# Loading a batch's attention operands from DRAM in two transfers with a doubled source instead of eight

## The chip, the cores and the metric

The kernel runs on one core of one Trainium2 chip. The metric is the device time of one execution in microseconds (us). Three runs of the kernel before took 4955.44, 4955.54 and 4960.33 us; the median is 4955.54 us.

A core has a matrix engine (TensorE, PE in the profile), three engines for elementwise work (VectorE or DVE, ScalarE or ACT, GpSimd or POOL) and a sync engine (SP). In this kernel SP alone issues the transfers between DRAM and the on-chip memory; 16 DMA engines carry them out.

## The reference

32 batches pass through four layers, with queries of shape 112 x 256 and a context of 375 x 256 per batch. The last layer (L3) is what matters here. It has 16 heads of size 16, a causal self-attention, a cross-attention over the context and a feed-forward block:

```python
def _mha(q_in, kv_in, wq, bq, wk, bk, wv, bv, causal):
    q = jnp.einsum('btc,hcd->bhtd', q_in, wq) + bq[None, :, None, :]
    k = jnp.einsum('bsc,hcd->bhsd', kv_in, wk) + bk[None, :, None, :]
    ...
    scores = jnp.einsum('bhtd,bhsd->bhts', q, k) * q.shape[-1] ** (-0.5)
    ...
x = x + _mha(ln1(x), ln1(x), ..., causal=True) @ m_proj_w + m_proj_b
x = x + _mha(ln2(x), x_e, ..., causal=False) @ c_proj_w + c_proj_b
x = x + relu(ln3(x) @ f_w1 + f_b1) @ f_w2 + f_b2
```

(The normalisations are written short here.)

## The kernel before

The kernel goes through nine sweeps over all batches: `l0x`, `l1s`, `l1x`, `l1f`, `l2x`, `l2f`, `l3s`, `l3x`, `l3f`. The first digit is the layer; `s` is self-attention, `x` cross-attention, `f` feed-forward. Batches are taken two at a time (`GB = 2`). Some sweeps run beside another one, staggered (`PAIRS`): `l2f` with `l3s`, and `l3x` with `l3f`.

Each sweep is cut into slots, and a slot into phases: scores and softmax, normalisation, transposition, product with the values, projection. `run` lays the slots of all sweeps in one sequence. `LAGS` says by how many slots a later phase trails the first. Preparatory steps (loading x, statistics, projections, loading operands) are "atoms"; `LEAD` says how many slots ahead of its unit each atom is due. For `l3s` the queries are loaded 3 slots ahead (`qload=3`), for `l3x` 4 slots (`qload=4`) and the keys 8 (`kload=8`). After this planning the framework's own scheduler, which works with a modelled timeline, decides the final order on each engine and the waits.

In L3, a value is kept as a high and a low part, so that a float32 product keeps its precision: a score is the sum of high x high, high x low, low x high and low x low. With heads of size 16 all four products are made in one matmul over 128 partitions. For each pair of heads `m`, the 128 partitions hold 8 blocks of 16 rows: two heads (`j`) and four combinations of query part and key part. Query rows of the other head of the pair are zeros.

To bring the operands into this form the kernel goes through DRAM. `queries_out` (line 854) writes the two parts of the projected queries of a batch pair into a DRAM buffer `dq_l3s` or `dq_l3x`, three buffers in turn, whose other rows were filled with zeros once. `queries_in` (line 871) reads a batch's queries back into a tile `qs` of 128 partitions x 2 x 8 x 112, with eight transfers (line 879): for each head parity `j` and each part `q`, the same 32 rows twice (`u`). The partitions so hold (high, high, low, low), in blocks of 32. `keys_out` (line 838) writes the keys to DRAM, and `keys_in` (line 845) reads them into two tiles `k6`, each by two transfers of 64 rows (line 852); the partitions hold (high, low, high, low).

`queries_in` is called once per batch in `l3s` and in `l3x`. `keys_in` is called once per batch pair in `l3s` (from the buffer `dk`, rows of 4 x 224 values) and once per batch in `l3x` (from `k3_...`, rows of 4 x 376 values, written during `l3s`). There are two `qs` buffers and five `k6` buffers.

The scores are then made on TensorE in line 1163 (`l3s`) and line 1111 (`l3x`):

```python
q, k = st["q"](2 * pr + j), st["k"](pr)
self.mark[s] = nc.tensor.matmul(sc[:, :TE], q, k, start=True, stop=True)
```

Other transfers run on the same SP queue in these sweeps. `keep_v` in line 521 stores the `l3x` values of each batch as two transfers of 125 rows, and line 1037 loads them again. Line 516 loads the kept context (`cd`), line 842 stores keys, line 868 stores queries, line 385 loads x, line 396 stores x. Elsewhere, lines 502 and 750 store and load values in 125 rows, line 552 stores the context in 128 rows, and line 269 loads eight bias vectors, each with its one row read twice (`partition_broadcast(2)`).

Of the kernel before, what the change touches and what calls it, by code (L numbers as in the profile page):

```python
# [8 lines left out]
F32 = mybir.dt.float32  # L9
# [52 lines left out]
class Kern:  # L62
# [775 lines left out]
    def keys_out(self, hl, W, tag, bufs):  # L838
# [3 lines left out]
            self.nc.sync.dma_start(d[:, j].rearrange("q d m n -> (d m) q n").bitcast(F32), hl[j].bitcast(F32))  # L842
        return d

    def keys_in(self, d, W):

        n = 4
        ts = [self.t([128, n, W], F32R, "k6") for _ in range(8 // n)]
        src = d.rearrange("q j d m n -> (q j d) m n")
        for ti, t in enumerate(ts):  # L850
            for u in range(2):
                self.nc.sync.dma_start(t[64 * u : 64 * u + 64].bitcast(F32), src[:, ti * n : (ti + 1) * n, :].bitcast(F32))
        return lambda m: ts[m // n][:, m % n, :]

    def queries_out(self, hl, s):
# [15 lines left out]
    def queries_in(self, d, i):  # L871

        t = self.t([128, 2, 8, S], F32R, "qs")
        for j in range(2):
            for q in range(2):
                src = d[i, j, q].rearrange("j d m n -> (j d) (m n)").bitcast(F32)
                for u in range(2):
                    o = 64 * q + 32 * u
                    self.nc.sync.dma_start(t[o : o + 32, j].rearrange("p m n -> p (m n)").bitcast(F32), src)
        return lambda hd: t[:, hd % 2, hd // 2, :]  # L880

    def queries_apart(self, i, c, bs):
# [717 lines left out]
```

## Time and profile before

| | |
|---|---|
| median of three runs | 4955.54 us |
| time of the profiled execution | 4969.08 us |
| span of the profiled execution | 4967.3 us |
| mean granted TensorE clock | 0.958 |
| TensorE busy, matmul / weight load | 4502.3 us (91%) / 4010.3 us (81%) |
| DVE / ACT / POOL busy | 73% / 69% / 43% |
| DMA: bytes, share of 16 engines (main queue) | 667.40 MB, 53.5% |
| transfers from `dq_l3s` / `dq_l3x` into `qs` | 256 / 256, 112.0 KB each |
| transfers from `dk` into `k6` | 64, 224.0 KB each |
| transfers from `k3_...` into `k6` | 128, 376.0 KB each |
| issue of one query transfer on SP, median | 419 ns |

How to read it: the page gives each engine's busy time as a share of the span, so an engine at 91% has little idle time left on average, though single stretches differ. The strips of digits cut the span into 40 slices of 124 us. The DMA share is the mean over 16 engines: a share of 0.31 can mean five engines that are busy all the time. GB/s is what all of them moved. In tile names buffer numbers are left out, so `k` stands for tiles of several kinds; `k<-dk` are the key loads of `l3s`, `k<-k` holds those of `l3x` (128) and the key stores before them (64). In the view of the DMA queues of a stretch, packets are counted by size. A row of a transfer is one packet, and completions are packets under 512 B; such views count the packets that start in the stretch, while issues are those of SP in it.

### The profile page before, as it was taken

The numbers are of one execution on the slowest core, as the hardware profiler recorded it, in microseconds if no ns is written. First come the engines' busy times: TensorE is split into PE (matmuls) and PEld (weight loads), VectorE is DVE, ScalarE is ACT, GpSimd is POOL, SyncE is SP. The second block draws the span as 40 slices with busy tenths as digits, with TensorE's granted clock in tenths as the row PEclk, the third lists the DMA queues.
The fourth block names the chain that finished last, engine by engine and source line by source line (L and its number), as shares of the span: only waits on it lengthen the run. The fifth ranks groups of instructions, "written<-read, shape, count | busy, mean of one in ns | idle before, by whom it ended". The sixth has DMA issues, their size and how long they took to land. (4 is left out here: it accounts for less than half of the span.)

```text
span 4967.3 us, 111690 instructions
## 1 busy us (share of the span) xinstructions
PE 4502.3 (91%) x37824; PEld 4010.3 (81%) x37824; DVE 3625.6 (73%) x9806; ACT 3409.2 (69%) x10644; POOL 2112.1 (43%) x3674
## 2 busy tenths in 40 slices
PE   5999999997778888888999999998998986899999
PEld 5888888886667777777999999997888886788878
DVE  4788888888887777776688888886555554677776
ACT  4788888887777766775577777774544544677776
POOL 4455555555443333332233333334333333566665
PEclk9999999999889999999999999999999998899999
DMA  4433333335666667667355555543656657666663
GB/s 102 124 85 86 84 80 88 86 87 127 135 141 134 138 128 135 129 143 143 110 142 143 142 142 143 143 128 108 196 172 198 189 182 212 174 160 165 160 165 85
DMA packets 585414, 674.53 MB, mean 136 GB/s; under 512 B 318688, under 2 KB 495056, under 8 KB 584656
## 3 DMA queue, kind: packets, MB, share of 16 engines
q1 hardware_dynamic: 584848, 667.40, 53.5%
q8 instruction: 305, 5.00, 0.4%
q14 instruction: 261, 2.14, 0.1%
HBM read 323.55 MB, written 173.02 MB: 100 GB/s over the span
## 5 line engine op out<-in xcount | busy, mean ns | idle before, releaser
L217 POOL TENSOR_SCALAR k<-k,sm 112x375 f32<-112x375 f32 (+1 forms) x1536 | 931.8, 619 | 1025.2 <-DVE sm L646 453.9
L200 ACT ACTIVATE k<-ps 125x336 f32<-125x336 f32 (+4 forms) x2005 | 912.8, 468 | 416.1 <-PE ps L237 190.1
L606 DVE TENSOR_REDUCE sm<-sc 112x1 f32<-112x375 f32 x1792 | 941.7, 539 | 151.8 <-PE sc L773 87.2
L612 ACT ACTIVATE k<-sc,sm 112x375 f32<-112x375 f32 x1536 | 879.5, 578 | 116.0 <-DVE sm L606 97.4
L664 PE MATMUL ps<-ident,k 112*125 112x112 f32 x4608 | 737.5, 277 | 19.8 <-issue 4.1
L664 PEld LDWEIGHTS ps<-ident,k 112*125 112x125 f32 x4608 | 649.9, 190 | 78.8 <-issue 41.8
L773 PE MATMUL sc<-k,qs 128*112 128x376 f32 x2048 | 540.0, 356 | 18.5 <-ACT k L612 8.3
L235 PE MATMUL ps<-w,k 128*125 128x256 f32 (+2 forms) x1344 | 435.6, 324 | 32.0 <-ACT k L612 17.9
L235 PE MATMUL ps<-h,w 128*128 128x224 f32 x1408 | 411.9, 300 | 44.0 <-DVE h L202 17.2
L695 DVE TENSOR_TENSOR k<-ps,k 64x376 fp32r<-64x376 f32 x640 | 350.0, 547 | 121.3 <-ACT k L200 106.0
L236 PE MATMUL ps<-h,w 128*128 128x224 f32 x1408 | 397.3, 284 | 0.7 <-DVE h L231 0.3
L237 PE MATMUL ps<-h,w 128*128 128x224 f32 x1408 | 395.0, 283 | 0.0
L236 PE MATMUL ps<-w,k 128*125 128x256 f32 (+2 forms) x1344 | 393.1, 292 | 0.0
L202 DVE COPY k<-ps 125x336 f32<-125x336 f32 (+2 forms) x619 | 289.0, 467 | 141.5 <-PE ps L237 65.2
L237 PE MATMUL ps<-w,k 128*125 128x256 f32 (+2 forms) x1344 | 391.9, 292 | 0.0
L235 PE MATMUL ps<-k,w 128*128 128x376 f32 x896 | 343.2, 383 | 37.2 <-DMA k<-cd 25.4
L213 POOL TENSOR_SCALAR k<-k,sm 112x375 f32<-112x375 f32 x256 | 164.5, 643 | 467.0 <-DVE sm L646 287.8
L795 PE MATMUL ps<-k,k 125*64 125x112 f32 (+1 forms) x4608 | 349.8, 296 | 3.7 <-DVE k L202 1.6
L773 PEld LDWEIGHTS sc<-k,qs 128*112 128x112 f32 x2048 | 304.4, 177 | 47.3 <-ACT k L612 23.5
L235 PEld LDWEIGHTS ps<-h,w 128*128 128x128 f32 x1408 | 275.0, 199 | 70.9 <-issue 28.9
L235 PEld LDWEIGHTS ps<-w,k 128*125 128x125 f32 (+2 forms) x1344 | 266.9, 199 | 72.7 <-ACT k L612 29.3
L612 ACT ACTIVATION_READ_ACCUMULATOR k<-sc,sm 112x1 f32 x1536 | 322.5, 210 | 0.0
(213 smaller groups left out, 12623.3 us busy)
## 6 DMA issues: line engine op xcount, KB each, us to landing
qs<-h SPq DMA_DIRECT2D x512, 224.0 KB
k<-k SPq DMA_DIRECT2D x192, 376.0 KB
k<-cd SPq DMA_DIRECT2D x64, 752.0 KB
vd<-k SPq DMA_DIRECT2D x128, 375.0 KB
k<-vd SPq DMA_DIRECT2D x128, 375.0 KB
qs<-dq_l3s SPq DMA_DIRECT2D x256, 112.0 KB
qs<-dq_l3x SPq DMA_DIRECT2D x256, 112.0 KB
x<-xd SPq DMA_DIRECT2D x224, 112.0 KB
```

The costliest lines, as they stand in the source:

```text
L200: self.nc.scalar.activation(out, in_, AF.Identity)
L202: self.nc.vector.tensor_copy(out, in_)
L217: self.nc.gpsimd.tensor_scalar(out, in_, by, 1.0, ALU.mult, ALU.mult)
L235: mm(out, lhs(0), rhs(0), start=start, stop=False)
L236: mm(out, lhs(0), rhs(1), start=False, stop=False)
L237: mm(out, lhs(1), rhs(0), start=False, stop=stop)
L606: nc.vector.tensor_reduce(nms[j], sc[j][:, :n], AX.X, ALU.max, negate=True)
L612: nc.scalar.activation(p[:, j, :n], sc[j][:, :n], AF.Exp, bias=nms[j], scale=1.0 if scale is None else scale, accum_out=sm[:, j : j + 1])
L664: self.nc.tensor.transpose(pst[:TB, a * S : (a + 1) * S], p[:, j, a * TB : (a + 1) * TB], self.ident[:S, :S])
L695: nc.vector.tensor_tensor(ks[o, j, :], pk[r, :TE], ks[r, j, :].bitcast(F32), ALU.subtract)
L773: nc.tensor.matmul(sc[:, :TE], qs[:, hd, q, bs], kk, start=q == 0, stop=q == 1)
L795: nc.tensor.matmul(o if gqa else o[:, mm, :], vq[:, a, hd * 64 : hd * 64 + 64], st["pt"][:, :, j, ta] if gqa else st["pt", mm][:, j, ta], ...
```

## The change

`keys_in` and `queries_in` exchange their layouts. The queries' partitions hold (high, low, high, low) in blocks of 32, the keys' (high, high, low, low). All four products are still there once. A new function `twice` makes one transfer whose source is the given DRAM rows with a dimension of 2 and step 0 put in front, so that the rows are read twice and fill the destination's partitions one copy after the other. `queries_in` then makes two transfers of 128 destination partitions, where it made eight of 32. `keys_in` still makes four of 64 destination partitions, each now of 32 source rows read twice.

```diff
+    def twice(self, out, src):
+
+        r, n = src.shape
+        self.nc.sync.dma_start(
+            out.bitcast(F32), src.bitcast(F32).unsqueeze(0).to_broadcast([2, r, n])
+        )
+
     def keys_in(self, d, W):
 
         n = 4
         ts = [self.t([128, n, W], F32R, "k6") for _ in range(8 // n)]
-        src = d.rearrange("q j d m n -> (q j d) m n")
         for ti, t in enumerate(ts):
-            for u in range(2):
-                self.nc.sync.dma_start(t[64 * u : 64 * u + 64].bitcast(F32), src[:, ti * n : (ti + 1) * n, :].bitcast(F32))
+            for q in range(2):
+                self.twice(
+                    t[64 * q : 64 * q + 64].rearrange("p m n -> p (m n)"),
+                    d[q].rearrange("j d m n -> (j d) m n")[:, ti * n : (ti + 1) * n, :].rearrange("p m n -> p (m n)"),
+                )
         return lambda m: ts[m // n][:, m % n, :]
...
         t = self.t([128, 2, 8, S], F32R, "qs")
         for j in range(2):
-            for q in range(2):
-                src = d[i, j, q].rearrange("j d m n -> (j d) (m n)").bitcast(F32)
-                for u in range(2):
-                    o = 64 * q + 32 * u
-                    self.nc.sync.dma_start(t[o : o + 32, j].rearrange("p m n -> p (m n)").bitcast(F32), src)
+            self.twice(t[:, j].rearrange("p m n -> p (m n)"), d[i, j].rearrange("q j d m n -> (q j d) (m n)"))
         return lambda hd: t[:, hd % 2, hd // 2, :]
```

## The prediction

> **What bounds the kernel now.** I read the page first, for the shape of the run.
>
> ```profile
> span 4967.3 us, 111690 instructions
> PE 4502.3 (91%) x37824; PEld 4010.3 (81%) x37824; DVE 3625.6 (73%) x9806; ACT 3409.2 (69%) x10644; POOL 2112.1 (43%) x3674
> DMA  4433333335666667667355555543656657666663
> ...
> qs<-dq_l3s SPq DMA_DIRECT2D x256, 112.0 KB
> qs<-dq_l3x SPq DMA_DIRECT2D x256, 112.0 KB
> ```
>
> TensorE is busy 91% of the span; the transfers use about half of the 16 DMA engines. The last two rows are the loads that the change rewrites. By the line's own view they are issued from 3456.5 to 4208.4 us (l3s) and from 4168.9 to 4894.4 us (l3x), so everything touched lies in the last third. I then asked for the stretches before, during and after.
>
> ```profile
> 3450.00:4180.00 730.00, 638.72 (x5200) 583.19 (x5199) 376.96 (x1052) 352.34 (x1433) 259.69 (x452) 0.92 0.63 192
> 4180.00:4895.00 715.00, 643.50 (x6718) 558.87 (x6718) 520.63 (x1469) 496.33 (x1594) 414.27 (x656) 0.94 0.64 166
> 4895.00:4967.00 72.00, 68.35 (x735) 63.99 (x734) 39.86 (x111) 45.60 (x141) 36.82 (x57) 1.00 0.09 28
> ```
>
> After the length, the columns are the busy us of PE, PE's weight load, DVE, ACT and POOL, then granted clock, DMA share, GB/s. TensorE is busy 87 to 90% here; the DMA share is 0.63, averaged over 16 engines. The waits of TensorE from 3450 us on say what a perfect query load could save:
>
> ```profile
> PE sc L1163 <- DMA qs<-dq_l3s: 36.9, 12, 5.1
> PE ps L235 <- DMA k<-cd: 25.4, 6, 10.9
> ```
>
> So 36.9 us is lost to queries, in 12 waits. This part is bound by TensorE, with DMA at two thirds of its capacity if every transfer uses all engines. Whether it does is seen in three stretches with few transfers in flight, in the view of the DMA queues.
>
> ```profile
> DMA packets 144, 0.77 MB, mean 220 GB/s; under 512 B 16, under 2 KB 16, under 8 KB 144
> ...
> q1 hardware_dynamic: 144, 0.77, 54.5%
> ...
> cd<-k SPq DMA_DIRECT2D x1, 752.0 KB
> ```
>
> That is 1140 to 1143.5 us: one store of 128 rows. 144 packets are 128 rows and 16 small ones, one for each engine that reports completion. The second is 1472.4 to 1477.6 us, one store of 125 rows (the transpose beside it was issued 0.45 us before the end):
>
> ```profile
> DMA packets 130, 0.38 MB, mean 74 GB/s; under 512 B 5, under 2 KB 5, under 8 KB 130
> ...
> q1 hardware_dynamic: 130, 0.38, 24.4%
> ...
> vd<-k SPq DMA_DIRECT2D x1, 375.0 KB
> ```
>
> 125 rows and 5 completions: five engines, since 5 is the largest divisor of 125 up to 16. The third is 191 to 200 us, in which the eight bias loads of line 269 are issued and land. Each reads one 1 KB row twice, through a source whose outermost count is 2 with step 0:
>
> ```profile
> DMA packets 814, 0.83 MB, mean 92 GB/s; under 512 B 35, under 2 KB 813, under 8 KB 813
> ...
> k<-in_ctx_dram SPq DMA_DIRECT2D x1, 375.0 KB
> xh<-in_L_xattn_a_bo_dram SPq DMA_DIRECT2D x2, 2.0 KB
> ```
>
> Eight loads on 16 engines would leave 128 completions. There are 35 in all, some of them of transfers issued earlier and of the 125-row context load. Two per load fit, sixteen do not. The number of engines follows the outermost count of the transfer.
>
> **The change, part by part.** TensorE, DVE, ACT and POOL issue the same numbers of instructions in the built program; the scheduler moves 459 of them on PE, 168 on DVE, 45 on ACT and 32 on POOL, all from the start of l3s on. SP issues 384 transfers fewer: 128 query loads for 512. Only SP issues transfers, so no other queue is passed.
>
> Saved issue time: 384 x 0.419 us (the median on line 879) = 161 us of SP, worth on the end only what it takes from the waits just shown, at most 36.9 us.
>
> The form of the transfers is what costs. In the built program the query load's source is 2 copies (step 0) x 64 rows x 896 values, its destination 128 partitions; a key load's source is 2 copies x 32 rows, its destination 64 partitions. The outermost source count is 2 for all of them, as in line 269. I therefore take two engines for every one, where the old forms (32 and 64 rows on both sides) divide by 16. What remains unshown: no load in this trace has a count of 2 on one side and 128 on the other, so the sides' roles are a rival below.
>
> The Trainium skill, "DMA: Bandwidth & Descriptors", section "Why a DMA increments its semaphore by 16 and not by 1", speaks to that gap: the engine count is the largest number up to 16 that divides the slowest non-1 count of both patterns. Its section "Rules for kernel authors" warns that a leading zero-stride broadcast of c copies confines the whole DMA to at most c engines, so by that page the sum is the two-engine one below; the same section's advice against splitting a load by partition halves would, taken alone, make it the 16-engine one. The 125-row and the two-copy loads above agree with the first rule; unequal counts no row here shows.
>
> Bytes on the two engines. Queries: 512 x 112 KB = 58.7 MB. Keys: 64 loads of 224 KB and 128 of 376 KB = 64.0 MB. Together 122.7 MB, 61.3 MB on each of two engines. From 3450 us on the kernel moves 261.0 MB (140.17 and 120.86 in the DMA views of 3450 to 4180 and 4180 to 4967 us); 138.3 MB are left, of which 128 transfers of 375 KB (v3, 125 rows, five engines) are 49.2 MB, 9.8 per engine, and the rest 89.2 / 16 = 5.6 MB per engine. I let the five include my two, since the bias loads, issued by 196.5 us behind a five-engine context load, were landing up to the end of that view. So 76.8 MB pass through each of the two.
>
> Rate of one engine. The 128-row store: 0.77 MB in 0.545 x 16 x 3.5 us of engine time = 25.2 GB/s. The 125-row store: 0.384 / (0.244 x 16 x 5.2) = 18.9. Two 125-row loads with little beside them (2564.7 to 2572 us, 0.74 MB at a share of 26.7%): 23.7. All of 4180 to 4967 us, all engines contending: 119.5 MB / (0.583 x 16 x 787) = 16.3. With two engines at work there is little contention, so I take the middle of 23.7 and 25.2, 24.45, and keep 16.3 and 25.2 as ends.
>
> 76.8 MB / 24.45 = 3139 us, against 1438 us in which these loads are issued today. Nothing covers the difference: TensorE has 1351 us of work there and would idle. Buffers (two for queries, five for keys) let a batch's loads run beside the batch before, so I add only the exchange that no buffer covers: per pair of batches and stage, the queries' write to DRAM must land before the read; in the chain of waits its pieces (2.77, 3.47, 4.06, 4.87 us) average 3.8, times 32 = 121 us. Below nothing this cannot be; its upper end is a quarter of the transfer time, if buffers also run dry.
>
> What queues behind: SP's issue stalls when the engines are full (eight query loads issued at 3464.06 us took 10.98 us, not 3.4), so x, v and the stores wait in SP's order, and with them all engines. The moved instructions I price at nothing: they sit inside the idle time; without that cover they are bounded by today's TensorE slack in the part, 1517 - 1351 = 166 us, either way.
>
> Sum: start 3456.5 + 3139 + 121 + tail after the last query load (4967.3 - 4894.4 = 72.9) = 6789 us of span. The profiled execution took 4969.08 us, 1.8 over its span and 13.5 over the median of 4955.54, so 6777, told as **6780 us**, 37% slower.
>
> **Rivals.**
>
> *Sixteen engines after all* (other sign). If the destination's 128 partitions decide the split, the loads spread evenly and the change does what it looks like: the 36.9 us, 3.7 of l3x and 1.3 of keys go, 4955.5 - 41.9 = 4914 us; half of it if the loads stay late for other reasons, 4935. For: no row has unequal counts. Against: the eight bias loads. It decides from eight engines up, where 122.7 / 8 + 15.4 = 30.7 MB at 24.45 take 1257 us, less than 1438.
>
> *Two engines at a lower rate.* At 18.9 GB/s: 4061 us, 7712 of span, 7700 told. At 16.3: 4709 us, 8350 told. For: copies of the same rows are read side by side, and loads contend today. Against: two engines leave the memory nearly idle.
>
> *Two engines, but hidden.* It needs 76.8 MB in 1438 us, 53 GB/s per engine, twice the best row. Excluded.
>
> *Two engines, v elsewhere.* (61.3 + 5.6) / 25.2 = 2655 us and no exchange: 6185 of span, 6170 told.
>
> **How the numbers follow.** Two engines near my rate: 65%. Lower rate (7300 and over): 14%. V elsewhere or better overlap (under 6400): 13%. Sixteen: 8%, of which 6% gain over 0.2%, 1% stay within 0.2% (what a measurement can tell from no change) and 1% lose. Chances: faster 0.06, same 0.01, slower 0.93. The range reaches from the end at 6170 to the 18.9 row's 7700: it leaves out the 8% and the slowest tenth.
>
> **What would show it.** Step 1: in any stretch of l3s or l3x the DMA share falls from 0.63 to some 0.2 and the rate from 190 to some 70 to 90 GB/s; small packets fall, as each new load leaves 2. Step 2: until 3450 us nothing changes. Step 3: TensorE's longest waits become query and key loads (over 1000 us in all), busy near 67%. Step 4: SP's issues on the new line take many us each. I am wrong if the share stays above 0.5 there, or if the part is under 2600 us long.

## The result: 37% slower, as forecast

The changed kernel takes 6800.87 us (median of four runs, 6788.95 to 6807.92), against 4956.51 us for the kernel before in the same session. The ratio is 1.3702, with a 95% interval of 1.3683 to 1.3721. The forecast was 6780 us, with a range of 6150 to 7700.

### The profile after

The page, its strips, and the rows of the query loads:

```profile
span 6787.2 us, 111215 instructions
PE 4675.5 (69%) x37824; PEld 4154.7 (61%) x37824; DVE 3631.5 (54%) x9806; ACT 3415.1 (50%) x10644; POOL 2111.0 (31%) x3674
...
PEclk9999999899999999999977777776666666666667
DMA  4433334666666645455423333332211111111111
...
DMA packets 574787, 674.47 MB, mean 99 GB/s; under 512 B 308064, under 2 KB 484432, under 8 KB 574032
...
qs<-dq_l3s SPq DMA_DIRECT2D x64, 448.0 KB
qs<-dq_l3x SPq DMA_DIRECT2D x64, 448.0 KB
```

Each digit of a strip now stands for 170 us. The first twenty slices, up to 3400 us, are those of before, drawn shorter. From there on the DMA share falls to 0.2 to 0.3 and then to 0.1, and TensorE falls with it to a third or a half. The packets under 512 B are the main line here. The page of before has:

```profile
DMA packets 585414, 674.53 MB, mean 136 GB/s; under 512 B 318688, under 2 KB 495056, under 8 KB 584656
```

So there were 318688 of them and now there are 308064, that is 10624 fewer. (Not all of them are completions: data rows of 448 bytes, 32768 in either trace, are counted too, and drop out of the difference.) The old kernel had 512 query and 192 key loads (704); the new one has 128 and 192 (320). If the old ones left 16 completions each and the new ones 2, the difference is 704 x 16 - 320 x 2 = 10624. It fits to the last packet.

The two engines can be seen at work in the view of the DMA queues from 5024 to 5039 us, in l3x, where only query loads move data (212 rows of 3584 bytes are the 0.76 MB):

```profile
DMA packets 214, 0.76 MB, mean 51 GB/s; under 512 B 2, under 2 KB 2, under 8 KB 214
...
q1 hardware_dynamic: 214, 0.76, 12.4%
```

12.4% of 16 engines are 1.98 engines. They move 51 GB/s, 25.5 GB/s each (0.76 MB in 0.124 x 16 x 15 us), and the two small packets are the completions of one load. The stretches of l3s and l3x (3452 to 4857 and 4857 to 6787 us) in the columns of the prediction:

```profile
3452.00:4857.00 1405.00, 691.87 (x5265) 627.96 (x5263) 387.22 (x1076) 362.29 (x1475) 262.83 (x456) 0.72 0.31 102
4857.00:6787.00 1930.00, 828.80 (x7333) 720.33 (x7332) 553.62 (x1546) 534.41 (x1685) 444.56 (x703) 0.66 0.17 60
```

The same stretches of work took 751 us (3452 to 4203) and 764 us (4203 to 4967) in the kernel before. The number of instructions per engine is the same; the time is not work. What TensorE waits for from 3440 us on:

```profile
PE sc L1116 <- ACT k L612: 427.9, 35, 46.3
PE sc L1168 <- DMA k<-dk: 427.0, 17, 44.2
PE sc L1116 <- DMA qs<-dq_l3x: 256.2, 33, 15.3
PE ps L664 <- ACT k L200: 205.7, 6, 35.5
PE ps L235 <- DMA k<-cd: 176.9, 16, 24.3
```

Three of these rows name transfers (with `k<-v`, 130.6 us, and `qs<-dq_l3s`, 48.4 us, such rows come to 1039 us). The two rows that name ScalarE lead to transfers as well, since ScalarE was itself waiting. The page's rows of these two lines (behind the second bar stand the idle time of the engine before them and what ended most of it):

```profile
L612 ACT ACTIVATE k<-sc,sm 112x375 f32<-112x375 f32 x1536 | 878.6, 577 | 818.3 <-DMA dq_l3x<-k 474.5
L200 ACT ACTIVATE k<-ps 125x336 f32<-125x336 f32 (+4 forms) x2005 | 912.5, 468 | 686.9 <-DMA dq_l3x<-k 249.7
```

`dq_l3x<-k` are the stores of the queries to DRAM, for which the same two lines waited 4.9 and 5.5 us before. They stand in SP's order behind the loads. One case: SP stands 12.91 us at a load (line 848) from 5522.65 us on and only then issues the stores (line 877); the last piece of them takes 13.95 us from 5542.48 us on, and TensorE, which had waited 33.7 us for ScalarE, goes on at 5557 us. SP shows how a load now holds up what stands behind it (the line's own view: ns, shortest, median, longest issue):

```profile
L848 SPq DMA_DIRECT2D k<-k x128: 482/4276/14544, 4688.8 to 6685.3; - x128
...
L848 SPq DMA_DIRECT2D qs<-dq_l3x x64: 482/3918/12643, 4800.6 to 6695.3; - x64
```

A query issue took 419 ns in the median before. Now SP stands some 4 us at an issue in l3x, and up to 14.5. The 704 query and key loads of before held SP for 330 us in all, the 320 of now for 1460 us: 384 issues fewer cost far more of SP's time.

### The profile page after: what moved, and what is told of

Same layout as the page of the kernel before. It is cut to its first block, busy times and chain, and to the rows that moved or that the text cites. A ratio compares the mean times of both kernels' runs of the same rounds, so it can differ in the third digit from the quotient of the medians.

```text
span 6787.2 us, 111215 instructions
## 1 busy us (share of the span) xinstructions
PE 4675.5 (69%) x37824; PEld 4154.7 (61%) x37824; DVE 3631.5 (54%) x9806; ACT 3415.1 (50%) x10644; POOL 2111.0 (31%) x3674
## 2 busy tenths in 40 slices
DMA packets 574787, 674.47 MB, mean 99 GB/s; under 512 B 308064, under 2 KB 484432, under 8 KB 574032
## 4 chain that ended last, share of the span: by engine, by line
DMA 28%; PE 23%; SPq 12%; DVE 2%; issue 1%; ACT 0%; POOL 0%; ACTq 0%; DVEq 0%; POOLq 0%
DMA qs<-dq_l3x 10%; SPq L848 7%; DMA qs<-dq_l3s 5%; DMA dq_l3x<-k 4%; PE ps L664 3%; PE ps L235 3%; DMA k<-dk 3%; PE ps L236 3%; PE ps L237 3%; PE sc L773 2%; PE ps L795 2%; DMA out_dram<-x 2%; SPq L1042 1%; PE ps L1080 1%; SPq L385 1%
## 5 line engine op out<-in xcount | busy, mean ns | idle before, releaser
L664 PE MATMUL ps<-ident,k 112*125 112x112 f32 x4608 | 785.5, 290 | 221.3 <-ACT k L200 208.2
L664 PEld LDWEIGHTS ps<-ident,k 112*125 112x125 f32 x4608 | 696.3, 203 | 286.2 <-issue 252.7
L1116 PE MATMUL sc<-k,qs 128*112 128x376 f32 x512 | 208.5, 429 | 716.6 <-ACT k L612 427.9
L1116 PEld LDWEIGHTS sc<-k,qs 128*112 128x112 f32 x512 | 100.5, 205 | 741.6 <-ACT k L612 446.0
L773 PE MATMUL sc<-k,qs 128*112 128x376 f32 x2048 | 540.2, 356 | 19.4 <-ACT k L612 9.3
L231 POOL TENSOR_TENSOR ot<-s,ot 128x224 fp32r<-128x224 f32 x224 | 152.6, 683 | 1139.9 <-ACT ot L200 633.1
L235 PE MATMUL ps<-k,w 128*128 128x376 f32 x896 | 348.7, 389 | 189.1 <-DMA k<-cd 176.9
L235 PE MATMUL ps<-h,w 128*128 128x224 f32 x1408 | 425.0, 309 | 53.3 <-DVE k L931 17.5
L1168 PE MATMUL sc<-k,qs 128*112 128x112 f32 x512 | 100.1, 326 | 475.4 <-DMA k<-dk 427.0
L236 PE MATMUL ps<-h,w 128*128 128x224 f32 x1408 | 411.6, 294 | 0.6 <-DVE h L231 0.3
L237 PE MATMUL ps<-h,w 128*128 128x224 f32 x1408 | 409.1, 293 | 0.0
L1168 PEld LDWEIGHTS sc<-k,qs 128*112 128x112 f32 x512 | 83.0, 214 | 491.7 <-issue 248.2
L222 ACT ACTIVATE s<-ps,vec_L_xattn_b 128x224 f32<-128x224 f32 x128 | 58.2, 459 | 596.8 <-PE ps L237 596.5
```

What stands on the lines that cost most here:

```text
L235: mm(out, lhs(0), rhs(0), start=start, stop=False)
L236: mm(out, lhs(0), rhs(1), start=False, stop=False)
L237: mm(out, lhs(1), rhs(0), start=False, stop=stop)
L664: self.nc.tensor.transpose(pst[:TB, a * S : (a + 1) * S], p[:, j, a * TB : (a + 1) * TB], self.ident[:S, :S])
L773: nc.tensor.matmul(sc[:, :TE], qs[:, hd, q, bs], kk, start=q == 0, stop=q == 1)
```

## The experiments

Theory A is that of the prediction: a transfer runs on as many engines as the outermost count of its source allows, 2 in the changed kernel, and the time follows from the bytes on the fullest engine. Theory B puts the loss on the new layout, on the moved instructions or on fewer and larger transfers. Theory C says that any source with a step of 0 is slow.

### The layout without the doubled source

```diff
-                self.twice(
+                self.copies(          # keys: 8 transfers of 32 rows per batch
...
-            self.twice(t[:, j]...
+            self.copies(t[:, j]...    # queries: 4 transfers of 64 rows per batch
+    def copies(self, out, src):
+        r = src.shape[0]
+        for u in range(2):
+            self.nc.sync.dma_start(out[r * u : r * u + r].bitcast(F32), src.bitcast(F32))
```

> The new layout kept, but each doubled transfer is made as two plain ones (queries 4 of 64 rows per batch, keys 8 of 32 rows), so no source has a copy count in front. Theory A (a doubled source with the 2 outermost runs on two engines): 16 engines again, DMA share above 0.5 and some 160 to 200 GB/s from 3450 us on, time within 1% of 4956 us. Theory B (the cost is in the layout, in the moved instructions of the other engines or in fewer and larger query transfers): stays near 6800 us, or at least above 5500.

Measured: 5009.19 us, ratio 1.0102 (1.0077 to 1.0127). The 37% are gone with the doubled source, so the new layout does not make them. The page has 317664 small packets, 1024 fewer than before, which is 704 x 16 - 640 x 16 for the 640 loads of this run: sixteen engines each. Fewer and larger transfers, the other part of theory B, are settled by the run with the copies inside below. The 1.0% that is left is a little over what theory A allowed. It lies in l3s, whose last key store is issued at 4236.9 us instead of 4200.4. There TensorE's wait for the context loads grew; its row from 3440 us on, 25.4 us before, is now the one below. Why it grew was not tried.

```profile
PE ps L235 <- DMA k<-cd: 93.4, 15, 10.8
```

### Only the queries, only the keys

```diff
# only the queries doubled: the keys' call becomes plain
-                self.twice(
+                self.copies(
...
# only the keys doubled: the queries' call becomes plain
-            self.twice(t[:, j]...
+            self.copies(t[:, j]...
```

> Only the queries use the doubled source; the keys are plain loads of 32 rows. Theory A: 58.7 MB instead of 122.7 lie on two engines. With 9.6 MB of evenly spread bytes and 9.8 MB of the 125-row transfers that is 48.8 MB per engine, 1995 us at 24.45 GB/s, told 5640 us (5450 to 5850). Theory B': the number of query issues is at fault: as the changed kernel, 6800 us.

> Only the keys use the doubled source; queries are plain loads of 64 rows. Theory A: 64.0 MB on two engines. In l3s 7.3 MB of keys, 6.2 of the rest and 4.9 of 125-row transfers are 18.5 MB per engine, 755 us, about what that part takes from TensorE; in l3x 24.6 + 2.9 + 4.9 = 32.4 MB, 1325 us instead of 715. Told 5600 us (5450 to 5800), nearly all of the loss behind 4200 us. Theory B (layout or order): no such split by part.

Measured: 5794.87 us for the queries (1.1686, 1.1651 to 1.1721) and 5927.75 us for the keys (1.1954, 1.1919 to 1.1989). Either half alone makes a large loss, in the direction that the bytes say, and the small packets fit two engines for the doubled half and sixteen for the plain one (4864 and 6784 fewer than before, 704 x 16 - 128 x 2 - 384 x 16 and 704 x 16 - 256 x 16 - 192 x 2). But both times lie above the forecasts: by 155 us, inside the range, and by 328 us, outside it. The parts show where. I take the issue of the last key store of l3s as its end, in the view of line 842 (last number ahead of the semicolon), for the kernel with doubled keys:

```profile
L842 SPq DMA_DIRECT2D k<-k x64: 359/388/5197, 3496.2 to 4470.3; - x64
```

It was 4200.4 us before and 4855.0 in the changed kernel. So with doubled keys l3s takes some 1018 us, where the two engines have 755 us of transfers and the part took 748 us before. l3x takes 1460 us, against 1398 by bytes and tail. The forecast had nearly all of the loss in l3x; 270 us of it lie in l3s.

Part of both misses is the rate of an engine, which the length of each packet in the trace's records gives. With doubled queries, the query rows of l3x (3584 bytes, the only ones of that size there) took 164 ns on average, 21.8 GB/s, against 145 ns and 24.8 GB/s in the changed kernel. At 21.8 GB/s the 48.8 MB of the forecast take 2239 us, not 1995. With doubled keys, the key rows of l3x (6016 bytes) took 258 ns, 23.4 GB/s; at that rate 32.4 MB take 1385 us, with the tail about the 1460 measured. What makes l3s some 263 us longer than its 755 us of transfers is not shown: rows of keys and of queries have the same size there and can't be told apart.

### The copies inside instead of in front

```diff
     def twice(self, out, src):
         r, n = src.shape
         self.nc.sync.dma_start(
-            out.bitcast(F32), src.bitcast(F32).unsqueeze(0).to_broadcast([2, r, n])
+            out.bitcast(F32), src.bitcast(F32).unsqueeze(1).to_broadcast([r, 2, n])
         )
...
             for q in range(2):
-                self.twice(t[64 * q : 64 * q + 64]..., d[q]...)
+                self.nc.sync.dma_start(
+                    t[64 * q : 64 * q + 64].rearrange("p m n -> p (m n)").bitcast(F32),
+                    d.rearrange("c j d m n -> (j d) c m n")[:, :, ti * n : (ti + 1) * n, :].rearrange("p c m n -> p c (m n)").bitcast(F32),
+                )
```

Queries now hold each row in two neighbouring partitions, keys hold their two parts in neighbouring partitions. The number of transfers and their bytes are those of the changed kernel; the queries still have a step of 0.

> The same number of transfers as the changed kernel (2 for queries, 4 for keys) and the same bytes, but the copies lie inside: the query source is 64 rows, each read twice in a row (rows outermost, then the 2 with step 0); keys are 32 rows times their two parts. The partitions hold the same four products in another order. Theory A: the outermost count is 64 or 32, so all 16 engines work: 4920 to 4970 us; with the query waits (36.9 us) gone at best 4915. Rival C (any source with a step-0 dimension, wherever it stands, is slow, for instance because the same row is read twice side by side): above 5600 us.

Measured: 4907.94 us, ratio 0.9891 (0.9864 to 0.9917); run again later, 4917.07 us and 0.9913 (0.9889 to 0.9937). Theory C falls: the step of 0 does not slow a load that has 64 rows in front of it. What was left of theory B falls too, since the number and the bytes of the transfers are those of the changed kernel. Its page has 312544 small packets, 6144 fewer than before, which is 704 x 16 - 320 x 16: all sixteen engines report. This version is about 1% faster than the kernel before, 12 us under the range that was expected, and close to the 4914 us that the prediction worked out for sixteen engines. TensorE's waits for query loads, 36.9 + 3.7 us before, have shrunk to these two rows:

```profile
PE sc L1168 <- DMA qs<-dq_l3s: 0.8, 1, 0.8
...
PE sc L1116 <- DMA qs<-dq_l3x: 0.5, 1, 0.5
```

### Four and eight copies in front

```diff
-            out.bitcast(F32), src.bitcast(F32).unsqueeze(0).to_broadcast([2, r, n])
+            out.bitcast(F32), src[: 2 * r // 4].bitcast(F32).unsqueeze(0).to_broadcast([4, 2 * r // 4, n])
```

and the same with 8 in place of 4.

> The changed kernel with 4 copies of half the source rows in front (a step-0 count of 4): the same transfers and bytes, but each destination row gets a row of the first half, so the low parts (queries) or the second head of each pair (keys) are left out of the scores. Theory A (the engine count is the outermost count): four engines. 122.7 / 4 + 15.4 = 46.1 MB per engine, 1885 us at 24.45 GB/s, told 5520 us (5350 to 5750); 4 completions per transfer; DMA share about 0.3 and rate near 100 GB/s in l3x. Rival C (a step-0 dimension in front costs the same whatever its count): 6800 us. Rival D (any small count makes the transfer fall to a fixed two engines): 6800 us.

> As the kernel with 4 copies, with 8 copies of a quarter of the source rows; three quarters of the rows are left out of the scores. Theory A: eight engines, 122.7 / 8 + 15.4 = 30.7 MB per engine, 1257 us, less than TensorE's 1351 us in this part, so the loss is all but gone: 4900 to 5100 us. Rivals C and D: 6800 us.

Measured: 5621.85 us with four copies (1.1325, 1.1255 to 1.1394) and 5167.11 us with eight (1.0409, 1.0334 to 1.0484). With two copies it is 6801, with 64 or 32 rows in front 4908. Rivals C and D, that the count does not matter or that a small one always gives two engines, are out. The page with four copies:

```profile
DMA packets 575427, 674.47 MB, mean 120 GB/s; under 512 B 308704, under 2 KB 485072, under 8 KB 574672
```

318688 - 308704 = 9984 = 704 x 16 - 320 x 4: four completions for each load. With eight copies the page has 309984 small packets, 8704 fewer, which is 704 x 16 - 320 x 8. Four copies came out 100 us over the forecast and inside its range; eight came out 67 us above its range. The views of l3x show why, first with four copies, then with eight:

```profile
4437.00:5625.00 1188.00, 765.22 (x7330) 665.47 (x7326) 552.33 (x1545) 532.88 (x1684) 442.18 (x701) 0.77 0.28 98
4250.00:5156.00 906.00, 727.42 (x7322) 635.21 (x7320) 551.02 (x1545) 532.92 (x1684) 442.43 (x702) 0.88 0.44 129
```

A busy engine moved 98 / (0.28 x 16) = 22 GB/s with four copies and 129 / (0.44 x 16) = 18 with eight. It was 22 with two (60 GB/s at a share of 0.17) and 16 in the kernel before (152 at 0.59, from 4203 to 4967 us). The forecast for eight took 24.45 GB/s, so that 1257 us would hide behind TensorE's work. At 18 GB/s its 30.7 MB are some 1700 us, and the part took 1704 us (3452 to 5156).

### Where the gain of the copies inside comes from

```diff
# cut by destination partitions: 4 transfers of 64 partitions per batch
+            for q in range(2):
+                self.twice(t[64 * q : 64 * q + 64, j]..., d[i, j, q].rearrange("j d m n -> (j d) (m n)"))
# cut by columns: 4 transfers of 128 partitions, half a row each
+            for w in range(2):
+                n = slice(4 * S * w, 4 * S * w + 4 * S)
+                self.twice(t[:, j]...[:, n], d[i, j]...[:, n])
```

> The kernel with the copies inside once more, as a yardstick for the two variants beside it: 4890 to 4920 us, some 1% under the kernel before.

> Copies inside as in the yardstick, but the query transfers are cut by destination partitions: 4 per batch, each of 64 partitions (32 rows, each twice in a row), 16 engines each. Theory G (the gain of the yardstick over the kernel before comes from loads that fill all 128 partitions at once, against the old loads of 32): part of the gain is lost, 4920 to 4945 us. Theory H (it comes from fewer issues on SP): the same as the variant cut by columns, 4910 to 4930 us for both.

> Copies inside as in the yardstick, the query transfers cut by columns: 4 per batch, each of 128 partitions and half a row (1792 bytes). Theory G: as the yardstick, 4890 to 4920 us. Theory H: as the variant cut by partitions, 4910 to 4930 us.

Measured: 4917.07 us (0.9913) for the yardstick, 4959.03 us (1.0006, 0.9992 to 1.0021) cut by partitions, and 4925.64 us (0.9936, 0.9914 to 0.9957) cut by columns. The two variants make the same number of query transfers and differ by 0.7%; their intervals do not touch. So the gain is not in the number of issues alone (theory H). It goes with the 128 destination partitions (theory G), and cut into 64 nothing of it is left, less than I had forecast; cut by columns the time is 6 us above theory G's range. The 33 us between the two variants stand in TensorE's waits for transfers, from 3440 us on cut by partitions:

```profile
PE ps L235 <- DMA k<-cd: 43.7, 6, 10.8
...
PE sc L1169 <- DMA qs<-dq_l3s: 23.1, 7, 4.7
```

and cut by columns:

```profile
PE ps L235 <- DMA k<-cd: 31.8, 7, 8.8
...
PE sc L1172 <- DMA qs<-dq_l3s: 0.5, 1, 0.5
```

These rows differ by 34.5 us. That the width is the reason is argued, not shown: the order in which the scheduler put the instructions was not held fixed, and the width does not order the rates. In l3x a query row of 3584 bytes took 207 ns on average in the yardstick and 229 ns cut by partitions, but 201 ns in the kernel before, whose loads have 32 partitions. What limits the loads of 64 partitions was not tried.

### More lead in l3s

```diff
-        l3s=dict(load=10, stats=8, apply=7, q=7, qload=3, k=6, ...
+        l3s=dict(load=13, stats=12, apply=11, q=11, qload=5, k=10, ...
```

> The changed kernel with more lead in l3s: queries and keys projected 11 and 10 slots ahead instead of 7 and 6, query loads 5 instead of 3. In the changed kernel l3s took 1405 us, where its bytes on the two engines (31.3 MB at 24.45 GB/s) give 1280. If the rest is a wait for loads that start too late (427 us of TensorE's waits there name the key loads), l3s falls to about 1300 and the time to some 6690 us. If SP's fixed order behind the long issues sets it, no gain: 6800 us or more. l3x stays at some 1930 us either way.

Measured: 6796.71 us in one run, no gain. The wait for the key loads did shrink, and another took its place. TensorE from 3440 us on:

```profile
PE ps L235 <- DMA k<-cd: 591.9, 21, 43.7
...
PE sc L1168 <- DMA k<-dk: 46.0, 2, 38.6
```

427.0 us of `k<-dk` became 46.0, and 176.9 us of `k<-cd` became 591.9. l3s ends at 4870.2 us instead of 4855.0. Only which load TensorE stood at has changed; issuing earlier did not shorten the part. The packet records of the changed kernel say why: in its l3s, fewer than two packets of the main queue are in flight for only 60 of the 1405 us, so there was little waiting of the two engines to take away. More buffers for queries or keys were not tried.

## Why the prediction was right, step by step

- **Two engines.** Right, shown by the count of completions, by the share of 12.4% and by the series over 2, 4, 8 and 16 engines. The gap that the trace of before left open, a source count of 2 against 128 or 64 destination partitions, is closed: the smaller count decides, here always the source's. That the five engines of a 125-row transfer include the two, which the sum assumed, shows as well: between the first and the last query issue five packets of the main queue are in flight for 312 us and seven for 26 us. With five other engines it would be seven. The Trainium skill, "DMA: Bandwidth & Descriptors", section "Rules for kernel authors", says that a leading zero-stride broadcast of c copies confines a DMA to at most c engines. The runs agree for c of 2, 4 and 8. The advice of the same section to use one 128-partition transfer rather than two halves agrees as well, once the outermost count allows it: 4917.07 us with one transfer and 4959.03 us with two halves. The reason that it gives was not tested here.
- **Bytes.** Right: the page still moves 674.47 MB, 674.53 before, and the loads have the sizes used in the sum.
- **Rate of one engine.** 24.45 GB/s was taken. 25.5 was measured where only the two work, and over all of l3x 24.8 for query rows and 23.4 for key rows. The term was right within 5%, and the rivals at 18.9 and 16.3 are out. It holds for two engines with little beside them: the runs with half of the loads on sixteen engines (21.8 for the query rows) and with eight copies (18) were forecast with it and came out longer.
- **Time in which the two engines wait.** 121 us were taken for the exchange of queries through DRAM. Query loads were issued from 3450.2 to 6695.3 us, 3245 us in all. In the packet records at least two packets of the main queue are in flight for 3121 us of these, and fewer for 125 us; 3139 and 121 were forecast. (Two packets in flight need not be on the two engines, so this is an estimate.) That the 121 fit so well is in part luck. They are 32 stores of queries at the 3.8 us of the chain of before; in the chain of the changed kernel such a piece took 13.95 us at 5542 us, while loads issued earlier still ran beside it.
- **The sum.** In the span it missed by 2 us (6789 against 6787.2). The 21 us between the forecast and the median come from the profiled executions: the one before was 13.5 us over its median, which the forecast took off, and the one of now is 12 us under its own.
- **Start and tail.** Start as said, 3450.2 us against 3456.5. From the last query issue to the end it took 91.9 us, not 72.9.
- **What would show it.** The share fell to 0.31 in l3s and 0.17 in l3x (0.2 was said), the rate to 102 and 60 GB/s (70 to 90 was said): right in the mean, without the difference between the parts. l3s also stores 125-row and 128-row transfers, which still use 5 and 16 engines. TensorE is 69% busy, against 67 forecast. SP's issues of some 4 us are as said. One sign came out otherwise: the rows of TensorE that name query and key loads come to 732 us, not over 1000, and the longest row names ScalarE, which waited for the stores of the queries. What the prediction said of transfers that queue behind in SP's order covers this.
- **Layout and moved instructions at nothing.** Right within about 1%: the layout with plain copies gave 1.0102, with the copies inside 0.989.
- **The rival of sixteen engines** was priced at 4914 us. The kernel that reaches sixteen took 4908 and 4917.

## What to carry to other kernels

Before you save transfers by a broadcast source, look at the outermost count of both sides as the instruction carries them: that count, not the bytes or the partitions, sets how many of the 16 engines work, and the completions in a profile (packets under 512 B) tell it at once. Put the rows outermost and the copies inside; the same merging of eight loads into two that lost 37% then gained 1%. In a sum, take the rate of an engine from a row with as many engines at work: 24.45 GB/s held for two and was too high for eight.

## What was not expected of the hardware

The granted TensorE clock was lower where TensorE had less to do. In l3x it is 0.95 with TensorE 91% busy in the kernel before, 0.88 with 80% with eight copies, 0.77 with 64% with four, and 0.66 with 43% in the changed kernel. There the score matmuls of l3x took 429 ns on average, against 376 before, and TensorE's busy time in the whole run rose from 4502.3 to 4675.5 us for the same instructions. What this costs in the end was not tried.

A busy engine moved less the more engines the loads ran on. A query row of 3584 bytes in l3x took 145 ns on average with the loads on two engines, 157 on four, 206 on eight, and 201 to 235 on sixteen, in the kernel before and in the versions with sixteen above. So eight engines were less than twice as fast as four.
